# Loads of the FFN weights under test, and stores of their sums: issued by GpSimd on its own queue instead of by SyncE

## The chip, the cores and the metric

The kernel runs on one core of a Trainium2 chip. The metric is the device time of one execution in microseconds (us); the time before is the median of three runs. A profile is one further execution, recorded on the chip: its span is the time from the first to the last instruction of the program.

## The reference

One transformer layer on x of 8 images x 512 rows x 256 columns, all in float32. In the attention part q and k are normed to length 1 for each head:

```python
x = x + layernorm(attention(layernorm(x)))
x = x + layernorm(ffn(layernorm(x)))

# attention: 16 heads of 64
q = l2norm(x @ w_q) * exp(scale); k, v = split(x @ w_kv); k = l2norm(k)
out = softmax(q @ k.T) @ v; return out @ w_out + b_out

# ffn: hidden size 1024; every weight is -1, 0 or 1, with a scale for each output
h = silu((x @ w1.T) * w1_s) * ((x @ w2.T) * w2_s)
h = gelu((h @ h1.T) * h1_s); h = gelu((h @ h2.T) * h2_s)
return (h @ w3.T) * w3_s
```

## The kernel before, in words

The kernel has two stages. The attention stage takes the images one after the other (b = 0 to 7) and in each its 8 pairs of heads (p). The q and k of an image are made in two halves (hf) of four pairs each: TensorE multiplies (`qp`, `kp`, line 411), ScalarE copies the result to `qT`, `kT` (line 422) and squares it (427). For each pair the scores `s` (541) are made, ScalarE takes their exponential `e` (555), VectorE sums the exponentials (566, `es`), and TensorE multiplies them with v (`po`, 586).

Before the scores of a half can be made, its q and k are divided by their norms. This is a chain through five engines and memory, once for q and once for k of every half (`norms_step`, from line 445): TensorE sums the squares (`pn_q`, `pn_k`, 456), ScalarE copies them (`nd_q`, `nd_k`, 480), SyncE issues a DMA that folds them into a small tile (`nf_q`, `nf_k`, 462), VectorE bounds them from below (488), GpSimd raises them to the power -1/2 (312), VectorE multiplies those of q with the heads' scale (495), SyncE stores them to memory (`nq`, `nk`, 502) and reads them back spread over the partitions with two DMAs (`spread_q`, `spread_k`, 470), and VectorE multiplies `qT`, `kT` with them (512). A similar, shorter round through memory gives the reciprocals of the softmax sums for every two pairs (`fold` 651, `r` 657, `rden` 662, used in 691).

Beside the attention the kernel tests the FFN's weights. `looked_at` (line 848) loads 128 rows of a weight matrix, 512 KB, into a tile `w` of a pool with four buffers (854), and VectorE gathers in `loose` whether any value differs from -1, 0 and 1 (861 and 866). `weight_sums` (885) does this for two blocks of rows of h1 or h2, forms four sums and differences of their halves on VectorE (898) and stores each, 256 KB, to memory (902). There are 16 such loads for h1 and h2 and 32 stores, and 6 more loads for w1, w2 and w3. The FFN stage, which begins at about 1020 us, multiplies blocks of h1 and h2 with seven products in place of eight and reads the stored sums for this (`wb_S`, 1235); the kernel falls back to another function where the test or a bound on the scores fails. After the tests the same four buffers take w1 and w2 for the FFN (`wr`, 918, loaded by GpSimd).

The order of the instructions on each engine is not written out by hand. Each step is given to a planner (`Steps.add`) with its engine, an estimated length, what it reads, writes and which buffers it takes, and a `lag`, the time until what it started has landed. TensorE's steps stay in the order in which they were given; on every other engine the planner (`issue`, line 84) takes among the steps that are ready the one whose due time is the earliest. A step that issues a DMA counts on the engine that issues it ("sync" or "pool"), and each engine then works its list off in order: an instruction that has to wait holds up all that stands behind it. Every DMA reports its landing on one of eight semaphores that its queue uses in turn.

Of the kernel before, what the change touches and what calls it, by code (L numbers as in the profile page):

```python
# [139 lines left out]
def tile_fast(  # L140
# [41 lines left out]
    nc = tc.nc  # L182
# [116 lines left out]
    def bounded():  # L299
# [7 lines left out]
        writes=[("escale", 0)], earliest=landed["escale"],  # L307
# [6 lines left out]
    def tile_of(pool, shape, tag, key, dtype=F32, bufs=None):  # L314
        T[key] = pool.tile(shape, dtype, tag=tag, bufs=bufs, name="_".join(str(k) for k in key))
        return T[key]
# [473 lines left out]
    for b in range(B):  # L790
# [5 lines left out]
        if b:  # L796
# [3 lines left out]
            n = b - 1 + NX  # L800
# [18 lines left out]
    def reloads(c):  # L819
# [22 lines left out]
    sums_dram = {  # L842
        (n, k): dram.tile([P, NH // 2, HALF], F32, tag=f"s{n}{k}", name=f"s{n}{k}")
        for n in range(2)
        for k in range(1, 5)
    }

    def looked_at(n, k, rows_of, after):

        w = ("w", n, k)  # L850

        def load():
            dst = tile_of(wp, [P, HID], "w", w)
            nc.sync.dma_start(
                dst if len(rows_of.shape) == 2 else dst.rearrange("p (c n) -> p c n", n=D), rows_of
            )

        def marked(i):

            a, y = T[w][:, ts(i, S)], ("y", n, k, i)  # L860
            nc.vector.scalar_tensor_tensor(
                tile_of(sump, [P, S], "y", y, bufs=1), a, 0.0, a, ALU.is_equal, ALU.add
            )

        def gathered(i):
            nc.vector.scalar_tensor_tensor(
                loose, T["y", n, k, i].bitcast(I32), 0x3F800000, loose,
                ALU.bitwise_xor, ALU.bitwise_or,
            )

        steps.add(
            "sync", 0.1, load, lag=9.0, writes=[(w, 0), (w, 1)], takes=[("wrows", 4, w)], earliest=after
        )
        for i in range(2):
            y = ("y", n, k, i)
            steps.add(
                "dve", 0.72, lambda i=i: marked(i), reads=[(w, i)], writes=[(y, 0)],
                takes=[("y", 1, y)],
            )
            steps.add(  # L880
                "dve", 0.72, lambda i=i: gathered(i), reads=[(y, 0)], writes=[("loose", 0)]
            )
        return w

    def weight_sums(n, k, w_rows, after):

        w1, w2 = (
            looked_at(n, c, w_rows[:, c, :], after) for c in (k, k + NH // 2)
        )


        def summed(j, op, x, y, into):
            def part(q):
                return T[q[0]][:, ts(q[1], HALF)]

            steps.add(
                "dve", 0.72,
                lambda: nc.vector.tensor_tensor(part(into), part(x), part(y), op),
                reads=[x, y], writes=[into],
            )  # L900
            steps.add(
                "sync", 0.1, lambda: nc.sync.dma_start(sums_dram[n, j][:, k, :], part(into)),
                reads=[into], writes=[(("stored", n, k, j), 0)], lag=7.0,
            )

        summed(1, ALU.add, (w1, 1), (w2, 1), (w2, 1))
        summed(3, ALU.subtract, (w1, 0), (w1, 1), (w1, 1))
        summed(2, ALU.subtract, (w2, 1), (w1, 0), (w1, 0))
        summed(4, ALU.subtract, (w2, 0), (w1, 0), (w2, 0))
# [12 lines left out]
    def weight_work():  # L922
        after = 60.0
        for n, w_rows in enumerate((h1_rows, h2_rows)):
            for k in range(NH // 2):
                yield lambda n=n, k=k, r=w_rows, a=after: weight_sums(n, k, r, a)
        for n, w_rows in enumerate((w1_rows, w2_rows)):
            for c in range(ND):
                yield lambda n=n, c=c, r=w_rows: looked_at(2 + n, c, r[:, c, :], after)
        for c in range(NH // NT):  # L930
            yield lambda c=c: looked_at(4, c, w3_rows[:, c * NT : (c + 1) * NT, :], after)
        for c in range(ND):
            for k in range(2):
                yield lambda k=k, c=c: load_gate(k, c)
# [1068 lines left out]
```

## Time and profile before

| What | Value |
|---|---|
| Time before, median of three runs (lowest, highest) | 1626.56 us (1623.93, 1628.23) |
| The profiled execution, its own time | 1627.83 us |
| Its span | 1626.0 us |
| TensorE busy, granted clock | 1603.5 us (99%), 0.997 |
| VectorE, ScalarE, GpSimd busy | 1023.9, 878.2, 487.5 us |
| DMA queue of SyncE (q1): moved, share of the 16 DMA engines | 95.71 MB, 22.3% |
| DMA queue of GpSimd (q0): moved, share | 61.87 MB, 12.3% |
| Loads of line 854: number, first to last issue | 22, at 59.0 to 267.1 us |
| Stores of line 902: number, first to last issue | 32, at 86.9 to 236.7 us |
| Loads `wr` of line 918 (GpSimd) | 4, at 260.0 to 283.8 us |

Lines are those of the kernel before. Engines are named PE (TensorE), DVE (VectorE), ACT (ScalarE), POOL (GpSimd) and SP (SyncE); a q behind a name means the engine's sequencer, which issues DMAs. In a timeline a row gives start and length in us, engine, line, operation, what is written and what is read, how many instructions were merged, and in brackets the engine's idle time before and what ended it. In a list of waits a row gives who waited for what, the total in us, how often and the longest. A row of a DMA queue gives packets, megabytes and the time its packets took as a share of 16 engines over the stretch. In the chain of waits a row gives start, length and what the chain then consisted of.

### The profile page before, as it was taken

How to read it: one execution, taken by the hardware profiler on the slowest of the kernel's cores; microseconds unless marked ns; L12 is line 12 of the kernel's file. 1: busy time of each engine (PE TensorE's matmuls, PEld its weight loads, DVE VectorE, ACT ScalarE, POOL GpSimd, SP SyncE). 2: the span in 40 equal slices, each digit the busy share in tenths (PEclk: the TensorE clock that was granted, in tenths of full speed). 3: DMA queues.
4: the chain of work that ended last, by engine and by line, in shares of the span. 5: the costliest groups of instructions: out<-in, count | busy, mean ns of one | idle time of the engine just before them, and what ended most of it. 6: DMA issues, size and time to landing. Idle time of an engine off the chain costs nothing.

```text
span 1626.0 us, 18855 instructions
## 1 busy us (share of the span) xinstructions
PE 1603.5 (99%) x6808; PEld 915.9 (56%) x6808; DVE 1023.9 (63%) x1708; ACT 878.2 (54%) x1343; POOL 487.5 (30%) x356
## 2 busy tenths in 40 slices
PE   9999999999999999999999999999999999999997
PEld 4333443443443443353353354788888888888886
DVE  3587886454354363363363375869786987879686
ACT  4665445545545535635535634466566646654663
POOL 4211303302212122122112120447155426534451
PEclk9999999999999999999999999999999999999999
DMA  6446555222133122122122131444414532452440
GB/s 177 119 139 169 151 181 132 68 66 67 41 79 67 42 79 67 41 74 63 43 75 66 29 92 27 143 129 132 147 61 143 156 113 79 141 157 66 132 154 29
DMA packets 91042, 159.91 MB, mean 98 GB/s; under 512 B 23868, under 2 KB 39484, under 8 KB 86844
## 3 DMA queue, kind: packets, MB, share of 16 engines
q1 hardware_dynamic: 71324, 95.71, 22.3%
q0 software_dynamic: 18912, 61.87, 12.3%
q8 instruction: 55, 0.90, 0.2%
q10 hardware_dynamic: 704, 1.05, 0.2%
q14 instruction: 47, 0.39, 0.1%
HBM read 140.26 MB, written 17.56 MB: 97 GB/s over the span
## 4 chain that ended last, share of the span: by engine, by line
PE 82%; DVE 3%; issue 2%; DMA 2%; POOL 1%; ACT 1%; SPq 0%; DVEq 0%; POOLq 0%
PE g L1256 25%; PE s L541 12%; PE po L586 11%; PE p L1182 6%; PE pa L711 6%; PE kp L411 5%; PE qp L411 5%; PE vp L387 5%; PE py L1370 3%; PE pd L609 2%; DMA spread_k<-nk 1%; POOL nf_k L312 1%; DMA nk<-nf_k 1%; PE pn_q L456 1%; PE pn_k L456 1%
## 5 line engine op out<-in xcount | busy, mean ns | idle before, releaser
L555 ACT ACTIVATE e<-s 128x1024 f32<-128x1024 f32 x256 | 248.2, 1021 | 120.8 <-PE s L541 120.3
L541 PE MATMUL s<-qT,kT 64*128 64x512 f32 x1024 | 255.8, 618 | 6.2 <-DVE kT L512 4.7
L586 PE MATMUL po<-e,v 128*64 128x512 f32 x1024 | 234.4, 600 | 0.0
L1256 PE MATMUL g<-h,wb_S 128*128 128x512 f32 x1024 | 234.3, 389 | 0.0
L312 POOL TENSOR_TENSOR nf_q<-nf_q,neghalf 128x32 f32<-128x32 f32 x16 | 88.0, 5499 | 439.2 <-DVE nf_q L488 439.2
L1256 PEld LDWEIGHTS g<-h,wb_S 128*128 128x128 f32 x1024 | 192.0, 188 | 39.8
L566 DVE TENSOR_TENSOR es<-es,e 128x1024 f32<-128x1024 f32 x128 | 156.6, 1224 | 87.9 <-ACT e L555 83.0
L541 PEld LDWEIGHTS s<-qT,kT 64*128 64x128 f32 x1024 | 88.0, 186 | 159.7 <-issue 115.0
L1256 PE MATMUL g<-h,wb_A 128*128 128x512 f32 x768 | 176.4, 389 | 0.0
L1256 PEld LDWEIGHTS g<-h,wb_A 128*128 128x128 f32 x768 | 144.0, 188 | 29.8
L586 PEld LDWEIGHTS po<-e,v 128*64 128x64 f32 x1024 | 68.0, 137 | 159.3 <-issue 158.8
L566 DVE TENSOR_TENSOR es<-e,e 128x1024 f32<-128x1024 f32 x64 | 78.3, 1223 | 119.3 <-PE pd L609 98.5
L1074 DVE TENSOR_TENSOR h<-C,h 128x512 fp32r<-128x512 f32 x112 | 129.4, 1211 | 3.9 <-ACT h L1064 3.8
L1074 DVE TENSOR_TENSOR h<-B,h 128x512 fp32r<-128x512 f32 x112 | 107.9, 1003 | 26.9 <-ACT h L1064 26.7
L312 POOL TENSOR_TENSOR nf_k<-nf_k,neghalf 128x32 f32<-128x32 f32 x16 | 89.0, 5562 | 117.1 <-issue 96.6
L387 PE MATMUL vp<-wkv_sb,aT 128*128 128x512 f32 x256 | 120.6, 602 | 0.0
L711 PE MATMUL pa<-wo_sb,oT 128*128 128x256 f32 x512 | 117.2, 382 | 0.0
L411 PE MATMUL kp<-aT,wkv_sb 128*128 128x512 f32 x256 | 115.8, 601 | 1.4 <-ACT kT L422 1.4
L1312 POOL TENSOR_TENSOR B<-B,B 128x512 f32<-128x512 f32 x64 | 102.0, 1621 | 43.7 <-DVE B L1213 38.8
L411 PE MATMUL qp<-aT,wq_sb 128*128 128x512 f32 (+1 forms) x272 | 114.3, 570 | 0.0
L711 PEld LDWEIGHTS pa<-wo_sb,oT 128*128 128x128 f32 x512 | 95.9, 190 | 31.1 <-issue 17.5
L681 ACT COPY oT<-po 128x512 f32<-128x512 f32 x64 | 37.5, 586 | 140.5 <-PE po L586 140.5
(131 smaller groups left out, 2079.2 us busy)
## 6 DMA issues: line engine op xcount, KB each, us to landing
wb_S<-s POOLq DMA_DIRECT2D x32, 1024.0 KB, 5.1
spread_q<-nq SPq DMA_DIRECT2D x32, 512.0 KB
spread_k<-nk SPq DMA_DIRECT2D x32, 512.0 KB
rden<-r SPq DMA_DIRECT2D x62, 256.0 KB
wb_A<-in_h1T_dram POOLq DMA_DIRECT2D x12, 1024.0 KB, 5.5
wb_A<-in_h2T_dram POOLq DMA_DIRECT2D x12, 1024.0 KB, 5.6
s<-w SPq DMA_DIRECT2D x32, 256.0 KB
w<-in_h1T_dram SPq DMA_DIRECT2D x8, 512.0 KB
```

The costliest lines, as they stand in the source:

```text
L312: nc.gpsimd.tensor_tensor(d, d, neghalf.to_broadcast([P, n]), ALU.pow)
L387: nc.tensor.matmul(pm, lhsT=T["aT", b][:, c, ts(t, P)], rhs=w[:, c, c0 : c0 + HALF], start=(c == 0), stop=(c == ND - 1),)
L411: nc.tensor.matmul(T[pm][:, cols], lhsT=w[:, c, c0 : c0 + P], rhs=T["aT", b][:, c, cols], start=(c == 0), stop=(c == ND - 1),)
L541: nc.tensor.matmul(T[s][:, h, :], lhsT=T[kT][hp, j, ts(jb, P)], rhs=T[qT][hp, j, :], start=True, stop=True,)
L555: lambda: nc.scalar.activation(tile_of(ep, [P, 2, S], "e", e), T[s], AF.Exp),
L566: nc.vector.tensor_tensor(T[t], T["e", b, p, 0] if jb == 1 else T[t], T["e", b, p, jb], ALU.add)
L586: nc.tensor.matmul(T[po][h * DH : (h + 1) * DH, :], lhsT=T[v][:, jb, c0 : c0 + DH], rhs=T[e][:, h, :], start=(jb == 0), stop=(jb == NT - 1),)
L711: nc.tensor.matmul(banks(), lhsT=T["oT", b, p][:, ts(t, P)], rhs=wo_sb[:, p, :], start=(p == 0), stop=(p == NP - 1),)
L1074: lambda: nc.vector.tensor_tensor(T[h][:, 1, c, :], T[raw][:, c, :], T[h][:, 0, c, :], ALU.subtract),
L1182: nc.tensor.matmul(T[ps[k]], lhsT=(w1r, w2r)[k][c][:, ts(o, P)], rhs=row_halves(b, i)[0][:, c, :], start=(c == 0 and i == 0), stop=(c == N ...
L1256: nc.tensor.matmul(T[to[o]], lhsT=T[w][:, c, ts(o, P)], rhs=T[h][:, i, c, :], start=(first and c == 0 and i == 0), stop=(c == NQ - 1 and i ...
L1312: lambda: (nc.gpsimd if T_ENGINE == "pool" else nc.vector).tensor_tensor(T[dst][:, c, :], T[x][:, c, :], T[y][:, c, :], ALU.subtract),
```

## The change

The 22 loads and the 32 stores are issued by GpSimd on its own queue. In the planner their steps count on "pool" with a length of 1.2 instead of on "sync" with 0.1, which are the planner's estimates in us; the lags stay. The planner puts them between GpSimd's other steps, and it moves VectorE's tests and sums among VectorE's other steps to fit; TensorE's and ScalarE's orders stay as they were.

```diff
@@ in looked_at
-            nc.sync.dma_start(
+            nc.gpsimd.dma_start(
                 dst if len(rows_of.shape) == 2 else dst.rearrange("p (c n) -> p c n", n=D), rows_of
             )
...
         steps.add(
-            "sync", 0.1, load, lag=9.0, writes=[(w, 0), (w, 1)], takes=[("wrows", 4, w)], earliest=after
+            "pool", 1.2, load, lag=9.0, writes=[(w, 0), (w, 1)], takes=[("wrows", 4, w)], earliest=after
         )
@@ in weight_sums, summed
             steps.add(
-                "sync", 0.1, lambda: nc.sync.dma_start(sums_dram[n, j][:, k, :], part(into)),
+                "pool", 1.2, lambda: nc.gpsimd.dma_start(sums_dram[n, j][:, k, :], part(into)),
                 reads=[into], writes=[(("stored", n, k, j), 0)], lag=7.0,
             )
```

In the order of the changed kernel all 54 stand on GpSimd. Around the powers of the norms (line 312) that order is: for image 1's first half, after the powers of q a load and two stores, then those of k; for its second half two loads and four stores between them; for image 2's first half three stores between them, and after those of k a load, a store and three loads.

## The prediction

> **What bounds the kernel now.** First the head of the page: TensorE is busy for all but 22.5 of 1626.0 us, so only time in which it stands still or runs slow can be won. Then the waits with TensorE as the one who waits:
>
> ```profile
> PE 1603.5 (99%) x6808; PEld 915.9 (56%) x6808; DVE 1023.9 (63%) x1708; ACT 878.2 (54%) x1343; POOL 487.5 (30%) x356
> ...
> PE s L541 <- DVE kT L512: 4.7, 3, 2.0
> ```
>
> Three waits, 4.7 us, are by far its largest; all are scores that wait for a half of the keys to be scaled. The timeline of TensorE places them (start, length, what, in brackets the idle time before):
>
> ```profile
> 131.02 3.65 PE L586 MATMUL po<-e,v 128*64 128x512 f32 x16
> 134.61 1.99 PE L541 MATMUL s<-qT,kT 64*128 64x512 f32 x8
> ...
> 142.27 3.07 PE L541 MATMUL s<-qT,kT 64*128 64x512 f32 x8 [2.04 <-DVE kT L512]
> 145.27 4.21 PE L586 MATMUL po<-e,v 128*64 128x512 f32 x16
> ...
> 212.19 1.99 PE L541 MATMUL s<-qT,kT 64*128 64x512 f32 x8 [1.25 <-DVE kT L512]
> ...
> 272.16 1.99 PE L541 MATMUL s<-qT,kT 64*128 64x512 f32 x8 [1.41 <-DVE kT L512]
> ```
>
> After the first wait the same groups take 3.07 for 1.99 and 4.21 for 3.65: 1.64 us more, at a granted clock of 0.76 over 142.3 to 149.5 us. After 1.25 and 1.41 us of idling nothing slows. So what can be won is 4.70 + 1.64 = 6.34 us. All three waits lie between 60 and 280 us, where the loads and stores of the change are issued. The rest of the idle time (start, the passage to the FFN at 1000 to 1100 us, the end) is untouched.
>
> Next the chain of waits before the first of them, and SyncE's issues there:
>
> ```profile
> 122.66 5.78 POOL nf_k L312
> 128.46 5.21 DMA nk<-nf_k
> 134.37 6.97 DMA spread_k<-nk
> ```
>
> ```profile
> 121.90 1.31 SPq L470 DMA_DIRECT2D spread_q<-nq  x2
> 123.31 0.55 SPq L902 DMA_DIRECT2D s<-w  x1
> 123.91 0.42 SPq L854 DMA_DIRECT2D w<-in_h1T_dram  x1
> ...
> 128.46 0.32 SPq L502 DMA_DIRECT2D nk<-nf_k  x1
> 133.72 1.26 SPq L470 DMA_DIRECT2D spread_k<-nk  x2
> ```
>
> The 16 KB nk takes 5.21 us. With no weights about it takes 1.4 (issued at 384.67, its reader at 386.13). At 128.46 it stands behind spread_q, a store and a 512 KB load of w that landed at 132.4; nk landed 1.3 us after that. The other two nk took 5.18 and 3.29 us, 0.2 us behind a load of w each.
>
> **What the Trainium skill says.** "DMA: Bandwidth & Descriptors", Queues, rings and completion order: descriptors of one queue are consumed in ring order on each DMA engine, and an engine takes turns between the queues it has work for. The first half agrees with nk above. The second doesn't hold in this trace: GpSimd's 512 KB load of 267.50 (line 918) moved nothing while SyncE's queue was busy. These are the queues' rows of the page asked for 267.4 to 271 and for 271 to 273.2 us (packets, MB, share):
>
> ```profile
> q1 hardware_dynamic: 700, 0.82, 108.1%
> ...
> q0 software_dynamic: 142, 0.52, 74.1%
> q1 hardware_dynamic: 267, 0.27, 43.6%
> ```
>
> spread_k, issued at 263.43, lay beside it and took 7.1 us from its second issue, against 6.8 to 7.2 with no load about. The same page, SWDGE vs HWDGE vs iDMA, puts descriptors of GpSimd's DMAs in software; here such a load lands in 3.6 us alone, SyncE's fastest in 3.2. "TensorE: Matmul & The Clock Gate", Part 1: an idle window of about 3.4 us halves the clock; the 1.64 us above agree in kind, after only 2.04 us of standing still. "SBUF — State Buffer", SBUF: two separate sides: a two-port VectorE operation keeps GpSimd from writing descriptors. No run here shows it.
>
> **The change part by part.** Removed: 22 loads (512 KB) and 32 stores (256 KB) from SyncE's queue, 0.33 to 0.6 us of issuing each, some 24 us over 220 us; SyncE computes nothing, so this alone is worth nothing. What counts is the ring behind them.
> - First wait (image 1, first half). spread_q's second half is issued at 122.59 and would land 6.9 us later, at 129.5 (it took 8.1 with two stores before it). nk, issued at 128.46, lands just behind, at 129.9 instead of 133.67: 3.8 us earlier, of which 2.04 are needed. The wait goes, and I take the 1.64 us of slow clock to go with it.
> - Second (image 1, second half). Without the load of 196.88 nk lands with rden, at 201.9 for 203.13: 1.2 us. Before it, nf_k's fold (issued 186.56) took 5.6 us behind two stores and a load; behind spread_q alone about 3. VectorE's new order puts a reciprocal and two multiplications, 1.5 us, ahead of its next step, so some 1 us of that is kept. 2.2 us against 1.25 needed.
> - Third (image 2, first half). Without the load of 257.22 nk lands behind spread_q (261.62) and a fold, at 262.0 for 263.35: 1.35 us against 1.41.
>
> Sum: 6.34 less a remainder of 0.4 us for the third and for small shifts: 5.9 us.
>
> Added: 54 issues on GpSimd. Rows of its own timeline give the price:
>
> ```profile
> 267.50 0.55 POOL L918 DMA_DIRECT2D wr<-in_w2T_dram  x1 [6.80 <-DVE y L861]
> ...
> 1030.18 0.58 POOL L1235 DMA_DIRECT2D wb_S<-s  x1
> 1030.78 0.57 POOL L312 TENSOR_TENSOR rsf<-rsf,neghalf 128x1 f32<-128x1 f32 x1
> ```
>
> 0.6 us from an issue to the next instruction; 54 x 0.6 = 32 us on an engine that is busy 18 to 24 us in each 100 there. What is queued behind them is the power of the norms (line 312, 5.4 to 5.8 us), for which VectorE (495), SyncE's store of nk and at last the scores wait. In the changed kernel's order a load and two stores stand between the powers of q and k of image 1's first half, two loads and four stores in its second half, three stores in image 2's first half: 1.8, 3.6 and 1.8 us. GpSimd idles there 3.15, 13.38 and 2.87 us now, so they fit, with 1.1 us to spare in the narrowest; without that cover they would cost their full 1.8 or 3.6. The waits in these issues are few: a store waits for its sum on VectorE, and each such sum stands ahead of the norm's own step in VectorE's order; a load waits for stores of the buffer before it, which land in 2.2 to 8 us and are issued longer ago than that where a power follows. I take nothing for them. Bounds: 0 if they are hidden; if an issue costs twice as much, 3.6 us against 2.87 and 3.15, 0.7 us late at most.
>
> Moved: VectorE runs the tests and sums later, and TensorE's and ScalarE's orders are the same. Up to 7 short steps (0.7 us each) move behind a chain's norm step, which delays the sums of exponentials behind them by 1.4 us at most; six buffers of e cover that (TensorE's own wait for exponentials is 0.3 us at most). Three loads go out at once near 63 us, beside the spread for the scores of 85 us, whose keys are ready at 77: 8 us of cover. The weights' own use comes at 1022 us, so their lateness is free.
>
> Sum against the profiled execution's own time: 1627.83 us (span 1626.0 and 1.8 around it) - 5.9 = 1621.9. That execution is 1.3 above the median 1626.56, so: 1626.56 - 5.9 = 1620.7 us.
>
> **The rivals.**
> 1. Only the first wait shrinks, or the clock still drops: the other two gains are small (1.2 and 1.35 us), and GpSimd's stores, started before spread_q, may hold the engines. Gain 2 to 4 us: 1622.5 to 1624.5.
> 2. Slower: the two queues share the engines fairly, as the skill says, and what now waits behind spread_k moves beside it. For: the trace has one case only, and in image 2's first half three loads and a store follow the power of k at once. A 512 KB load needs 1.44 us of all engines (128 packets of 0.18 us over 16), a store 0.7. spread_k of the third wait would then end 5 us later (3 x 1.44 + 0.7), that of the second 3.6 (two loads, a store); spread_q and spread_k of the first would lose 4.3 (two loads, two stores) against 3.8 won. Waits: about 1.41 - 1.35 + 5 = 5.1, 1.25 - 2.2 + 3.6 = 2.7 and 2.04 - 3.8 + 4.3 = 2.5, in all 10.3, and three drops of the clock, 4.9: 15.2 in place of 6.34, 8.9 us slower, 1635.5. At half of a fair share they come to 2.6, 0.9 and 0.4 us and one drop, 5.5: even, 1625.7. It decides from somewhat over half on. Against: the 7.1 us of spread_k above.
> 3. GpSimd becomes the brake: an issue holds it for over 0.95 us (2.87 / 3), so that the powers of k start late. At 2 us an issue, 6 us late less 3.15 or 2.87 idle is 3 us twice, against gains of 3.8 and 1.35: the first wait stays gone, the third becomes 3.2: about 1624; only with waits for stores as well does it end slower, at 1630.
> That the change doesn't do what it says can be left aside: all 54 issues stand on GpSimd in the order of the changed kernel.
>
> **How the numbers follow.** Full gain 55% (1619 to 1622.5), rival 1 18%, rival 2 17%, rival 3 10%. A measurement of this kernel tells about 0.3% (4.9 us) from no change: faster is below 1621.7, slower above 1631.4. Full gain falls below 1621.7 in 50 of its 55; rival 1 is all within 0.3%; rival 2 is slower in 15 and rival 3 in 8 of theirs, and the rest is within. Faster 0.50, same 0.27, slower 0.23. Predicted 1620.7. The range goes from 1618.5 (all 6.34 us and 1.7 us of scatter, as the three runs before show it) to 1630, which leaves out the worse part of rivals 2 and 3, some 18%. Cases of both signs being likely, the likeliest one's own range is 1619 to 1622.5.
>
> **What would show it.** Right: TensorE's wait for kT at most 0.5 us in all; nk landing within 2 us or just behind spread_q; groups of scores 1.99 us long throughout from 60 to 300 us; SyncE without lines 854 and 902; GpSimd's issues at 0.6 us. Wrong: spread_k longer than 7.5 us beside q0 packets (rival 2); a power of k that starts as soon as GpSimd's last issue ends (rival 3); a wait of TensorE elsewhere; the clock below full although the first wait is gone.

## The result, and the profile after

| | before | after |
|---|---|---|
| Time, median of four runs each (lowest, highest) | 1626.70 us (1623.93, 1628.23) | 1645.95 us (1644.33, 1647.44) |
| Ratio, 95% interval | | 1.0109 [1.0094, 1.0123] |
| The profiled execution: its own time, its span | 1627.83, 1626.0 us | 1645.88, 1644.0 us |
| TensorE busy, idle in the span | 1603.5, 22.5 us | 1608.3, 35.7 us |
| TensorE's waits for kT | 4.7 us, 3 | 17.3 us, 4 |

The kernel became 1.1% slower, 19.25 us, where 6 us were forecast to be gained. The page of the kernel after, and then its list of TensorE's waits (total us, how often, longest):

```profile
PE 1608.3 (98%) x6808; PEld 917.5 (56%) x6808; DVE 1024.4 (62%) x1708; ACT 878.7 (53%) x1343; POOL 519.5 (32%) x410
```

```profile
PE s L541 <- DVE kT L512: 17.3, 4, 7.1
```

The span grew by 18.0 us. The waits for kT account for 17.3 - 4.7 = 12.6 of it. TensorE is busy for 4.8 us more with the same 6808 instructions in the same order, which is slower running. The timeline of TensorE after shows both at once: the waits stand in the brackets, and the group behind three of them takes 3.6 to 3.8 us in place of 1.99.

```profile
147.79 3.78 PE L541 MATMUL s<-qT,kT 64*128 64x512 f32 x8 [7.15 <-DVE kT L512]
...
218.40 1.99 PE L541 MATMUL s<-qT,kT 64*128 64x512 f32 x8 [0.81 <-DVE kT L512]
...
283.26 3.65 PE L541 MATMUL s<-qT,kT 64*128 64x512 f32 x8 [6.30 <-DVE kT L512]
...
354.99 3.62 PE L541 MATMUL s<-qT,kT 64*128 64x512 f32 x8 [3.04 <-DVE kT L512]
```

They are the three places of before (2.04, 1.25, 1.41 us) and a new one, image 2's second half. Only the second shrank. Next comes the chain ahead of the first of them. GpSimd's row for the power of q before, and its timeline after:

```profile
113.69 5.82 POOL L312 TENSOR_TENSOR nf_q<-nf_q,neghalf 128x32 f32<-128x32 f32 x1 [50.67 <-DVE nf_q L488]
```

```profile
117.27 0.54 POOL L902 DMA_DIRECT2D s<-w  x1 [2.52 <-DVE w L898]
117.88 5.85 POOL L312 TENSOR_TENSOR nf_q<-nf_q,neghalf 128x32 f32<-128x32 f32 x1
123.69 0.59 POOL L854 DMA_DIRECT2D w<-in_h1T_dram  x1
124.29 1.07 POOL L902 DMA_DIRECT2D s<-w  x2
129.20 6.29 POOL L312 TENSOR_TENSOR nf_k<-nf_k,neghalf 128x32 f32<-128x32 f32 x1 [3.83 <-DMA s<-w]
```

and SyncE's issues beside it, before and after:

```profile
119.81 0.33 SPq L502 DMA_DIRECT2D nq<-nf_q  x1
120.19 0.63 SPq L462 DMA_DIRECT2D nf_k<-nd_k  x1
```

```profile
124.03 0.32 SPq L502 DMA_DIRECT2D nq<-nf_q  x1
124.40 0.64 SPq L462 DMA_DIRECT2D nf_k<-nd_k  x1
128.33 1.28 SPq L470 DMA_DIRECT2D spread_q<-nq  x2
...
135.52 0.32 SPq L502 DMA_DIRECT2D nk<-nf_k  x1
136.97 1.25 SPq L470 DMA_DIRECT2D spread_k<-nk  x2
```

What matters is who follows whom. The power of q ends at 123.7. Its end releases two things: the next instruction of GpSimd, a 512 KB load of w, at 123.69; and, by way of a short step on VectorE, nq on SyncE at 124.03. The load is 0.34 us ahead. nq, 16 KB, landed at 128.26, 0.2 us after the load (128.08): that is 4.23 us, where it took 1.40 before. The fold of nf_k, issued next, took 4.46 for 1.94. nk, which the change was to free, did become free: issued at 135.52, its reader at 136.97.

Step by step from SyncE's issues and the landings in the two traces, the last piece of spread_k landed 5.5 us later than before (146.86 for 141.34): the fold of nf_k issued later 4.21, the fold itself 2.52, from its landing to nk's issue 0.33, nk itself -3.81, spread_k 2.27 (9.24 for 6.97). The first term, 4.21, is the power of q starting at 117.88 for 113.69. GpSimd's store of 117.27 is off just before, but it held nothing up: the power's own input, the bound of nf_q on VectorE, was through only at 117.79. VectorE was late because it had stood still. Its rows before, and then after:

```profile
105.24 0.69 DVE L691 TENSOR_TENSOR oT<-oT,rden 128x512 f32<-128x512 f32 x1 [0.56 <-DMA rden<-r]
```

```profile
108.70 1.29 DVE L691 TENSOR_TENSOR oT<-oT,rden 128x512 f32<-128x512 f32 x2 [6.64 <-DMA rden<-r]
...
117.62 0.17 DVE L488 TENSOR_SCALAR nf_q<-nf_q 128x32 f32<-128x32 f32 x1
```

The round through memory of the softmax sums had met the same thing: r, 8 KB, issued at 99.36, took 4.44 us for 1.38 behind GpSimd's load of 98.85, so that rden was issued at 103.94 for 99.75, 4.19 us later.

### The profile page after: what moved, and what is told of

Same layout as the page of the kernel before. It is cut to its first block, busy times and chain, and to the rows that moved or that the text cites. A ratio compares the mean times of both kernels' runs of the same rounds, so it can differ in the third digit from the quotient of the medians.

```text
span 1644.0 us, 18850 instructions
## 1 busy us (share of the span) xinstructions
PE 1608.3 (98%) x6808; PEld 917.5 (56%) x6808; DVE 1024.4 (62%) x1708; ACT 878.7 (53%) x1343; POOL 519.5 (32%) x410
## 4 chain that ended last, share of the span: by engine, by line
PE 91%; DMA 4%; DVE 3%; ACT 1%; issue 1%; POOL 0%; SPq 0%; DVEq 0%; ACTq 0%
PE g L1256 25%; PE s L541 14%; PE po L586 13%; PE kp L411 7%; PE qp L411 6%; PE vp L387 6%; PE p L1182 6%; PE pa L711 6%; PE py L1370 3%; PE pd L609 2%; DMA spread_k<-nk 2%; PE pn_q L456 1%; PE pn_k L456 1%; ACT e L555 1%; DMA nf_k<-nd_k 1%
## 5 line engine op out<-in xcount | busy, mean ns | idle before, releaser
L541 PE MATMUL s<-qT,kT 64*128 64x512 f32 x1024 | 259.8, 626 | 18.8 <-DVE kT L512 17.3
L711 PEld LDWEIGHTS pa<-wo_sb,oT 128*128 128x128 f32 x512 | 95.9, 190 | 31.1 <-issue 17.3
```

Source lines behind the costliest of these rows:

```text
L541: nc.tensor.matmul(T[s][:, h, :], lhsT=T[kT][hp, j, ts(jb, P)], rhs=T[qT][hp, j, :], start=True, stop=True,)
L711: nc.tensor.matmul(banks(), lhsT=T["oT", b, p][:, ts(t, P)], rhs=wo_sb[:, p, :], start=(p == 0), stop=(p == NP - 1),)
```

## Experiments

Three theories are put against each other. Theory S: what GpSimd's queue has put on the DMA engines just before holds the chain's small transfers. Theory G: GpSimd works in order, and the waits inside its new issues (for VectorE's sums, for stores) hold the powers. Theory P: the planner's new order of VectorE's and SyncE's steps is to blame. Ratios are to the kernel before on the same chip, with 95% intervals.

### Plan and queue apart

The plan alone: SyncE issues, the steps count on pool with 1.2. The edit is against the kernel after; the store has the same one.

```diff
@@ in looked_at
-            nc.gpsimd.dma_start(
+            nc.sync.dma_start(
```

> The plan of the changed kernel (steps count on pool with 1.2), but SyncE issues the 54 DMAs: VectorE's order is exactly that of the changed kernel. Theory P: most of the 19.25 us stays, 1640 or more. Theory S: loads and stores lie in SyncE's ring again and hold the transfers of the norm chain that follow them there, in the order of the changed kernel; I expect 1626 to 1634, since a transfer in one ring behind a load lands as late as one beside it. Theory G: GpSimd's powers are free, 1624 to 1629, unless SyncE's own waits for sums now hold the chain's DMAs.

The queue alone: GpSimd issues, the steps count on sync with 0.1. The edit is against the kernel before, again with its like in the store.

```diff
@@ in looked_at
-            nc.sync.dma_start(
+            nc.gpsimd.dma_start(
```

> The plan of the kernel before (steps count on sync with 0.1), but GpSimd issues the 54 DMAs: VectorE's order is exactly that of the kernel before. Theory P: no loss, 1620 to 1628. Theory S: the transfers still lie beside the chain's, in the places that the plan of before gave them, 1632 to 1642. Theory G: the plan doesn't know that these steps stand in GpSimd's list, so powers stand behind them with their waits as well or worse: 1635 to 1650.

Measured: plan alone 1623.40 us, 0.9979 [0.9971, 0.9987], faster; waits for kT 0.3 us in all. Queue alone 1639.22, 1.0076 [1.0057, 1.0095]; waits for kT 11.5 us. P falls, and with the opposite sign: VectorE's and SyncE's new order is worth 0.2% by itself, better than any of the three theories said. There the three nk still stand behind stores and loads in SyncE's ring, but take 3.71, 2.58 and 3.38 us for 5.21, 5.18 and 3.29. The loss comes with the queue.

### Loads and stores apart

One half of the change each, with its planner's entry. For the loads, against the kernel before (for the stores it is the last hunk of the change alone):

```diff
@@ in looked_at
-            nc.sync.dma_start(
+            nc.gpsimd.dma_start(
...
-            "sync", 0.1, load, lag=9.0, writes=[(w, 0), (w, 1)], takes=[("wrows", 4, w)], earliest=after
+            "pool", 1.2, load, lag=9.0, writes=[(w, 0), (w, 1)], takes=[("wrows", 4, w)], earliest=after
```

> Only the 22 loads of line 854 go to GpSimd's queue, and their steps count on pool with 1.2; the 32 stores stay with SyncE. Before is 1626.7 us, after 1645.95 (+19.25). Theory S (the two queues come first-come on the DMA engines, so a load of GpSimd issued just ahead of a small transfer of the norm chain holds it): a load holds the engines twice as long as a store and most of the held transfers of the changed kernel stood behind loads, so about +12 us, 1639; nq or the fold of nf_k issued within 1 us of a GpSimd load takes 4 us or more. Theory G (GpSimd works in order, and its issues wait for VectorE's sums and for stores, ahead of the powers): the waits for sums are with the stores, so only the loads' waits for stores are left, +3 to +6 us, 1630 to 1633. Theory P (the planner's new order of VectorE's and SyncE's steps): anything, since that order is a third one; it is told apart by the two kernels that change only the plan or only the queue.

> Only the 32 stores of line 902 go to GpSimd's queue, and their steps count on pool with 1.2; the 22 loads stay with SyncE. Theory S: half as many bytes beside the chain, and nk stays behind loads in SyncE's ring as before: +4 to +7 us, 1631 to 1634. Theory G: the waits for sums are all there, so most of the loss is, +12 us or more, 1639; a power of nf_q or nf_k starts only when a store of GpSimd is off that waited for its sum on VectorE.

Measured: loads 1639.86 us, 1.0079 [1.0060, 1.0099]; stores 1629.72, 1.0016 [1.0005, 1.0026], less than S had said (1631) and far less than G (1639). Each has a plan of its own, so the same again with the plan of the changed kernel in both, where VectorE's and ScalarE's orders don't differ at all. Against the kernel after, the edit for the loads on GpSimd is the store's, and for the stores on GpSimd the load's:

```diff
@@ in summed
-                "pool", 1.2, lambda: nc.gpsimd.dma_start(sums_dram[n, j][:, k, :], part(into)),
+                "pool", 1.2, lambda: nc.sync.dma_start(sums_dram[n, j][:, k, :], part(into)),
@@ in looked_at
-            nc.gpsimd.dma_start(
+            nc.sync.dma_start(
```

> The complement with the same orders of VectorE and ScalarE: only the 22 loads are GpSimd's, the 32 stores are SyncE's. Theory S: 1636 to 1642, most of the loss; nq or nf_k's fold takes over 4 us behind a load of GpSimd that was issued within 1 us before it. Theory G: only the loads' waits for stores are left, 1624 to 1630.

> VectorE's and ScalarE's orders are exactly those of the changed kernel and of the kernel with the plan alone (1623.4 us); only the 32 stores are GpSimd's, the 22 loads are SyncE's. Theory S (transfers of the other queue that were issued first hold the chain's small ones): the stores are short, 1624 to 1629. Theory G (GpSimd's in-order waits for VectorE's sums hold the powers): the waits for sums are all here, so most of the 22.5 us between the plan alone and the changed kernel stays: 1635 or more.

Measured: loads 1638.76 us, 1.0094 [1.0069, 1.0119]; stores 1624.40, 0.9994 [0.9984, 1.0004]. From the plan alone (0.9979) the stores on GpSimd cost 0.15%, the loads 1.15%, and both together, the changed kernel, 1.30%: the terms add up, within intervals of 0.1 to 0.25% to each side, and nine tenths is the loads'. The waits for sums, G's main cause, lie with the stores. In the run with the loads alone nq took 3.47 and 3.53 us in image 1's two halves, each behind a load issued 0.33 and 0.34 us before it, and the fold of nf_k 3.32: held, but by less than the 4 us that S expected.

### The waits taken out of GpSimd's stores

```diff
+    ready = const.tile([P, HALF], F32, name="ready")
+    nc.vector.memset(ready, 0)
...
-                "pool", 1.2, lambda: nc.gpsimd.dma_start(sums_dram[n, j][:, k, :], part(into)),
+                "pool", 1.2, lambda: nc.gpsimd.dma_start(sums_dram[n, j][:, k, :], ready),
```

> The changed kernel, but each store takes its 256 KB from a tile of zeros that is always ready, so that it waits for no sum and no load waits for a store's reading; the sums that the FFN reads are left out. The bytes on GpSimd's queue are the same. Theory S: 1636 to 1648, the loss stays. Theory G: GpSimd is free for the powers, 1622 to 1630, and the power of nf_q of image 1's first half starts as soon as its bound is through on VectorE.

The sums that the FFN reads are left out here. Measured: 1653.44 us, 1.0175 [1.0158, 1.0192], slower still, and above S's 1648. The waits of TensorE:

```profile
PE s L541 <- DVE kT L512: 18.4, 4, 7.6
PE pd L609 <- DVE es L566: 3.1, 1, 3.1
```

The bound of nf_q was through at 120.92 and the power started at 121.01: nothing of GpSimd's stood before it, as G wanted, and the loss is all there. G falls. Without their waits the DMAs go out in bunches, four loads and four stores from 62.7 us on, two loads and four stores behind the power of k from 138.8 on.

### Another queue: ScalarE's

Against the kernel after, and likewise in the store:

```diff
@@ in looked_at
-            nc.gpsimd.dma_start(
+            nc.scalar.dma_start(
...
-            "pool", 1.2, load, lag=9.0, writes=[(w, 0), (w, 1)], takes=[("wrows", 4, w)], earliest=after
+            "act", 0.6, load, lag=9.0, writes=[(w, 0), (w, 1)], takes=[("wrows", 4, w)], earliest=after
```

> The 54 DMAs go to ScalarE's own queue (their steps count on act with 0.6). GpSimd issues none of them. Theory S: another queue on the same DMA engines, so the chain's transfers are held as beside GpSimd's: 1633 to 1645, with nq, folds or spreads 2 to 5 us longer behind such a load. Theory G: no wait stands before the powers, 1624 to 1630, unless ScalarE itself waits for sums: then TensorE's wait is for exponentials or copies of ScalarE, not for kT.

Measured: 1628.46 us, 1.0008 [0.9998, 1.0018]: the 1633 that S asked for was missed, and the figure lies in G's range. One wait of weight is left, 3.19 us at 270.11; its spread_k took 9.97 us from its second issue, beside a load that ScalarE had issued 0.65 us before its first. The fold of nf_k issued at 247.38 took 3.62 us beside a load that ScalarE issued even 0.18 us after it. So a load on this queue does the same where it falls beside the chain; in this plan few do, and none was issued within 1.6 us ahead of an nq of images 0 to 2. Whether the kind of queue matters as well is seen below.

### The disputed cost by itself

In images 3 to 7 of the kernel before, where no weights are tested, loads were added behind the powers (same values, no change of the output):

```diff
         steps.add("pool", 6.0, lambda: power(T[f], NF), writes=[(f, 0)])
+        if which == after:
+            for c in range(times):
+                steps.add(queue, 0.6, lambda c=c: again(c), reads=[(f, 0)])
```

> The kernel before, with additional loads of w1 and w2 rows over the same values in images 3 to 7, where no weights are tested: behind the power of q, so ahead of nq, GpSimd loads 512 KB (image 3, first half), 2 x 512 KB (3, second), 256 KB (4, first), 3 x 512 KB (4, second), 128 KB (7, first) and 4 x 128 KB (7, second); behind the power of k 512 KB (5, first) and 3 x 512 KB (5, second); ScalarE's queue loads 512 KB at image 6, in its list about the power of q (first half) and of k (second). Theory S: nq, 1.4 us alone, lands just behind the load of GpSimd issued before it: about 4.2 us behind 512 KB, 3 behind 256 KB, 2 behind 128 KB, and with 2 or 3 loads some 4.2 (if only the first is at the engines before it) up to 7; spread_k behind loads at the power of k takes 7 us plus 1.5 for each load. ScalarE's load holds a transfer issued just after it in the same way. Theory G: nq keeps its 1.4 us and spread_k its 7 everywhere; only the starts of powers move.

Issue to landing of nq (us), each with the load's issue 0.34 to 0.36 us ahead of it:

| Added ahead of nq on GpSimd's queue | nq | the (first) load landed ahead of nq's landing by |
|---|---|---|
| nothing | 1.40 to 1.44 | |
| 128 KB; 4 x 128 KB | 2.43; 2.52 | 0.17; 0.18 |
| 256 KB | 2.95 | 0.16 |
| 512 KB | 3.38 | 0.17 |
| 2 x 512 KB; 3 x 512 KB | 3.70; 3.83 | 0.18; 0.19 |

The case of 512 KB on GpSimd's timeline, on SyncE's, and in the DMA queues' rows (packets, MB, share of 16 engines) for 376 to 377.25 us:

```profile
374.64 0.59 POOL L504 DMA_DIRECT2D wr<-in_w1T_dram  x1
```

```profile
374.99 0.32 SPq L522 DMA_DIRECT2D nq<-nf_q  x1
...
378.42 1.28 SPq L470 DMA_DIRECT2D spread_q<-nq  x2
```

```profile
q0 software_dynamic: 101, 0.41, 101.2%
q1 hardware_dynamic: 92, 0.01, 12.4%
```

This is the whole effect on the transfer, without weights, sums or a plan about it: spread_q's issue comes 3.4 us after nq's. It costs no time here, for TensorE waits for no kT after 300 us in this run: the chains of images 3 to 7 have room for it. The last rows show how the two lie beside each other: 101 packets of the load to 92 of nq, nearly one for one (27 to 27, 19 to 19 and 26 to 26 in the last three quarters of a microsecond). By bytes nq is 1/32 of the load; by packets it is its equal, 128 of 128 bytes against 128 of 4 KB. G's "1.4 everywhere" is out. Two expectations of S were missed. Behind the powers of k one load had a lead of 0.07 us only: nk took 1.40 and spread_k 7.59; with three loads nk took 3.02 (2.12 there in the kernel before, where rden lies beside it) and spread_k 8.59, not 11.5: one of the three loads had landed when the second half of spread_k was issued, the others landed 1.1 and 3.7 us after that. And ScalarE's two loads were issued 0.23 us after one nq (1.40) and 3.5 us before one nk, which took 3.12 for 2.40 as rden, beside the load, came later. The one execution took 1628.95 us; 17 of the kernel before on the same chip took 1622.86 to 1629.26.

Then the same with ScalarE's queue ahead of nq, and with GpSimd's loads amid spread_q:

```diff
+        if which == where == "k":
+            loads_here()
         steps.add("pool", 6.0, lambda: power(T[f], NF), writes=[(f, 0)])
+        if which == where == "q":
+            loads_here()
```

> The kernel before with additional loads in images 3 to 7, as in the run with loads ahead of the chain. Behind the power of q, released by it: ScalarE's queue loads 496 KB (image 3 both halves, 5 second) and 128 KB (4 both), GpSimd's 512 KB (6 second) and 128 KB (7 second) as the measure. Behind the bound of nf_k and ahead of its power, while spread_q of image 5, 6 and 7's first halves is under way: GpSimd's queue loads 512, 3 x 512 and 512 KB. If a transfer of any other queue that was first is finished first, nq takes 3 to 3.8 us behind ScalarE's 496 KB and 2.4 behind 128 KB, like behind GpSimd's. If it is GpSimd's queue alone that does this, nq takes 1.4 to 1.9 behind ScalarE's. If the queues share once both have work, spread_q grows by 1.4 us for each load beside it and the load lands some 4 to 7 us after its issue. If who comes first is served first, spread_q keeps its 6.8 us from its second issue and the load lands behind it.

ScalarE's 496 KB went out 0.96, 1.57 and 1.58 us ahead of nq; nq landed 0.17, 0.16 and 0.17 us after them, 2.49, 3.18 and 1.83 us after its own issue (two of them less than the 3 to 3.8 expected, by the longer lead). Its 128 KB, 0.92 and 1.57 us ahead, left nq at 1.61 and 1.40. So it isn't GpSimd's queue alone. On GpSimd a short copy stood between the power and the load here, so that the load (512 and 128 KB) led nq by only 0.26 and 0.25 us, and nq took 1.41 and 1.40: it was first. Amid spread_q, 0.97 to 0.99 us after its second issue, the first load of each place landed 7.87, 6.90 and 6.67 us after its issue; spread_q took 9.27 us in the first place (6.81 there in the kernel before) and kept 6.59 and 6.40 in the other two, the one with three loads among them. What sets the first apart stays open. The one execution took 1627.75 us.

Last, more distance between load and nq, and loads from w3, which were meant to have four times as many packets:

```diff
+        if b >= 3 and which == "q":
+            steps.add("pool", 0.6, again, reads=[(f, 0)])
+            for _ in range({5: 2, 6: 2, 7: 4}.get(b, 0)):
+                steps.add(
+                    "dve", 0.12, lambda: nc.vector.tensor_scalar_max(T[f], T[f], 0.0),
+                    writes=[(f, 0)],
+                )
```

> The kernel before with an additional 512 KB load on GpSimd's queue behind the power of q, so just ahead of nq, in every half of images 3 to 7. In the first halves it is rows of w1 (128 packets of 4 KB, 8 for each of the 16 DMA engines, as many as nq has of 128 bytes), in the second halves rows of w3 (512 packets of 1 KB, 32 for each engine). In images 5 and 6 two idempotent steps on VectorE and in image 7 four lie ahead of nq, so that it is issued 0.2 us later for each of them. If the DMA engines take turns packet by packet between two queues that both have work, nq is through after 8 packets of the load for each engine: about 3.4 to 3.8 us in the first halves (with the load's last packet) and 1.9 to 2.5 in the second, while the load itself lands well after it. If a transfer that came first is finished first, nq lands just behind the load in both, 3.4 us or more.

As to packets the run says nothing: the trace records both kinds of load as 128 packets of 4 KB. Its distances do say something. With w1's load 0.87 us ahead nq landed 0.2 us behind it (2.98 and 2.84 us), and the rows of 622 to 624 us hold one queue:

```profile
621.17 0.59 POOL L494 DMA_DIRECT2D extra<-in_w1T_dram  x1
```

```profile
622.04 0.32 SPq L517 DMA_DIRECT2D nq<-nf_q  x1
...
625.08 1.28 SPq L470 DMA_DIRECT2D spread_q<-nq  x2
```

```profile
q0 software_dynamic: 111, 0.45, 73.5%
```

Not one packet of nq between 111 of the load. w3's load, whose issue takes 0.81 us for 0.59, comes too late at 0.34 us of lead (nq 1.43 and 1.41) and is in front at 1.09 (3.26 and 3.29). The one execution took 1624.28 us. So, far enough ahead, the load is finished first; nearly together, packets alternate and nq lasts as long as the load; not enough ahead, nq is first. Reckoned from the end of the load's issue, the three are cleanly apart in the traces of all runs, where GpSimd issued a load within 1.3 us ahead of an nq 35 times: where that end came 0.28 or 0.29 us before nq's issue (4 cases), nq landed 0.2 us behind the load; where it came 0.24 to 0.26 us after (21 cases), nq took 2.43 to 4.52 us; where it came 0.34 to 0.47 us after (10 cases), nq took 1.40 to 1.47. In the first two of these nq, 1.4 us alone, lasts until the load is through.

### The same DMAs on the same queue, but off the chain

The planner keeps GpSimd's loads and stores out of the time from each power of q to the landing of that half's spread_k; a copy of one column of spread_k on GpSimd makes the next of them wait for it.

```diff
+                if e == "pool" and held:
+                    ks = {k for k in ks if k not in self.heavy}
...
+            held = (held or k in self.holds) and k not in self.frees
...
+        if which == "k":
+            steps.frees.add(len(steps.all))
+            steps.add(
+                "pool", 0.3, lambda: nc.gpsimd.tensor_copy(seen, T[r][:, 0, 0:1]),
+                reads=[(r, j) for j in range(HP)],
+            )
```

> The changed kernel with its 54 DMAs on GpSimd's queue, but the planner puts none of them between the power of q and the landing of spread_k of any half: a small copy of a column of spread_k on GpSimd (one for each half, 16 in all) stands ahead of the next of them, so that they are issued when the norm chain has its data. Same bytes, same queue, same issues. Theory S: the loss goes, 1620 to 1627. Theory that any use of GpSimd's queue costs (its descriptors, its issues, waits for sums ahead of powers): most of the 19 us stays, 1636 or more.

Measured: 1621.02 us, 0.9972 [0.9964, 0.9980], faster than both kernels. GpSimd's timeline at image 1's first half, and the head of TensorE's waits, in which kT no longer stands:

```profile
121.32 5.42 POOL L317 TENSOR_TENSOR nf_k<-nf_k,neghalf 128x32 f32<-128x32 f32 x1 [4.08 <-issue]
135.71 0.18 POOL L520 COPY seen<-spread_k 128x1 f32<-128x1 f32 x1 [8.96 <-DMA spread_k<-nk]
136.25 0.61 POOL L868 DMA_DIRECT2D w<-in_h1T_dram  x1 [0.36 <-issue]
```

```profile
PE idle L1023 <- DVE idle L226: 1.6, 1, 1.6
PE s L555 <- ACT e L569: 1.5, 6, 0.3
PE kp L417 <- ACT kT L428: 1.4, 6, 0.2
```

Queue, bytes and number of issues are the changed kernel's, with 16 copies added; nq took 1.40 us, the fold 1.88, nk 1.40, spread_k 6.70. What cost the time in the changed kernel was the place of the DMAs, not their queue by itself. The planner moved VectorE's steps again here, so part or all of the gain over the kernel before may be its order's, as in the plan alone; the two intervals (0.9971 to 0.9987 and 0.9964 to 0.9980) overlap. Nor does this run by itself decide against G, since no DMA stands between the powers of a half here; the stores without waits do that.

## Why the prediction was wrong, point by point

- **The bound** was right: TensorE's waits for kT and the slow running behind them set what can be won. Where they were gone the span fell from 1626.0 to 1620.7 us (plan alone) and 1618.6 (held off): 5.3 and 7.4 us in single executions against the 6.34 named (by the medians' ratios 3.4 and 4.6 us of 1626.7). The Trainium skill's clock page ("TensorE: Matmul & The Clock Gate", Part 1) gives about 3.4 us of idling; here 3.04 us sufficed (the next group took 3.62 us for 1.99), and 0.81 didn't.
- **nk** was right: 1.40 us in each of the three halves, as alone.
- **The price of GpSimd's issues** was right: 0.54 to 0.6 us each (0.8 for the loads of w3), 519.5 - 487.5 = 32.0 us in all, hidden in the idle time before the powers of k: the one of 129.20 starts 0.15 us after its bound on VectorE. Their waits, taken at nothing, are not the cause (stores without waits).
- **VectorE's moves** were bounded at 1.4 us of loss at most. Together with SyncE's new order they are a gain of 0.2%, seen only with the plan alone.
- **The step that failed** is "The second doesn't hold in this trace": from one load that moved nothing beside spread_k I took it that GpSimd's queue doesn't take from SyncE's. That load had been issued after spread_k (267.50 against 264.09). The case fits a rule that who comes later waits, and I read it as who is on GpSimd's queue waits. In the changed kernel GpSimd's DMAs come first, by construction: the end of the power releases them directly, and nq only by way of VectorE, 0.34 us later. Nowhere did I ask what a DMA placed behind a power does to the transfer that the same power releases: nq took 4.23 us for the 1.40 that the sum left it.
- **Rival 2** had the right resource and the right sign, and said 1635.5 for 1645.95. It priced the spreads alone, by the time that the loads take of the engines. For the third wait that was right: spread_k there lasted 12.12 us, the 5 more that it forecast. The rows of after for 269.5 to 273.5 and for 273.5 to 276.5 us show it standing behind three loads and a store, then alternating:

```profile
q0 software_dynamic: 290, 1.06, 96.9%
...
q0 software_dynamic: 183, 0.67, 75.1%
q1 hardware_dynamic: 109, 0.22, 27.4%
```

  What it left out were the small transfers, nq, the fold and r, each 2.5 to 3.1 us longer in the first half, and image 2's second half, where a load and two loads `wr` now go out as the power of q ends (317.90 us) and TensorE waits 3.04 us. That makes waits of 17.3 us in place of the rival's 10.3. The three drops of the clock were as many as it said and cost somewhat more: 4.8 us on top of the 1.64 of before, 6.4 in all, against its 4.9.
- **Rival 3** falls with G; **rival 1** forecast a small gain and is out with the sign.
- Of the skill's sentence on turns ("DMA: Bandwidth & Descriptors", Queues, rings and completion order) this case shows both sides: turns, 101 packets to 92, where both queues had work from about the same moment; none, 111 to 0, where the load was 0.87 us ahead. I had dismissed it on one case. The section itself says that the turns go by packets; taken so, and counted in the packets of the trace, it would have priced nq at the load's length. Of the packets of 9 to 17 descriptors that it calls typical no run here shows anything.

## What to carry to other kernels

A transfer that is small in bytes can be long in packets, and in company it can last as long as the load beside it: before moving a load to another queue, look which transfers of the critical chain will be issued within a few microseconds after it, not only which ring it leaves. In one ring the order of the issues decides what the chain stands behind (nk, 5.21 us behind a load in the kernel before); on a second queue that order no longer helps, and an engine that feeds the chain and issues bulk loads behind its step puts the load's issue in front, here by 0.33 to 0.36 us. If bulk DMAs have to share an engine with a chain, hold them until the chain's last transfer has landed.

## What the runs showed of the hardware that was not expected

- A 16 KB transfer of 1.40 us took 2.43 us behind 128 KB, 2.95 behind 256 KB and 3.38 behind 512 KB of GpSimd's queue, and landed 0.15 to 0.2 us after it; behind 496 KB of ScalarE's queue it landed as closely after the load.
- Which one is first is settled within tenths of a microsecond: GpSimd's load of 512 KB with a lead of 0.26 us lost (nq 1.41), with 0.34 to 0.36 it shared, with 0.87 it was finished first. A load whose issue takes 0.76 to 0.81 us for 0.59 lost at 0.34: by the end of the issue the limit lies between 0.26 us (21 of 21 held nq) and 0.34 us (10 of 10 didn't) after nq's. The limit isn't the same for ScalarE's queue: there a load issued 0.27 us ahead of r (8 KB) held it for 3.24 us, and one issued 0.18 us after the fold of nf_k held that for 3.62.
- A load issued about 1 us after a spread of 512 KB twice landed only behind it, 6.67 and 6.90 us after its issue, and once landed 0.4 us ahead of it, the spread then taking 9.27 us (6.81 in that place without the load). What tells these apart stays open.
